# The fused third pass of a two-layer graph and mixture-of-experts kernel: another order of its steps

## The chip, the cores and the metric

The kernel runs on one core of one Trainium2 chip. The metric is the device time in microseconds (us) of one execution; lower is better.

## The reference

The input is 8192 tokens of 256 numbers (128 graphs of 64 nodes). Two layers follow each other, and each has a graph part and an expert part; both add to the running x:

```python
# layer 0
x = x + gnn0(layernorm(x), adj)              # adjacency, two dense layers
h = layernorm(x)                             # 64 experts, six for each token
x = x + layernorm(h + out_w @ mix(h)) * g + b
# layer 1
h = layernorm(layernorm(x))
x = x + relu((adj @ h) @ W_rel + b_rel + h @ W_root) + layernorm(x)   # the layer adds its own input
n = layernorm(x)
top2 = softmax(top_k(n @ Wg + bg, 2))        # 8 experts, two for each token
x = x + sum(top2[e] * ffn_e(n))
```

## The kernel before, in words

The work is done in four stages. The first computes the graph part of layer 0 and sends each token's row to a table in DRAM, six times, to the place of its expert. The second goes through that table in pages of 128 rows, multiplies each by its expert's matrix and scatters the products to the array r0y. The **fused pass**, which the change touches, gathers them again and does the rest of layer 0, all of layer 1's graph part, and the choice of experts of layer 1. The fourth stage goes through the table r1x, which the fused pass fills, in pages of 256 rows.

The fused pass works on 32 blocks of 256 tokens, each held as two tiles of 128 partitions. Its functions for a block b are:

- `load_y` (line 1010, two DMAs of 768 KB: the six products of each token) and `load3` (lines 1018, 1020, 610: xn1 and x1 of layer 0, 256 KB each, and the adjacency blocks).
- `fold` (line 1051, DVE) adds the last two of the six products to the first two; for blocks 0 to 7 it does nothing, and six are summed on PE in place of four. `mixture` (line 1030) sums and transposes the products on PE, 16 matmuls (24 in blocks 0 to 7), and ScalarE (ACT) copies the result out as accT (line 1033). `out_proj` (lines 1038, 1041) multiplies by out_w into po.
- `output` (A, 20 small steps): h = po + xn1 (line 1069), its statistics (lines 56, 59), a square root on ACT (line 36, bn_sd), a reciprocal (line 1075), the normalized h (1079), x2 (1083), its statistics, two more roots (std), reciprocals (1096 to 1101), and on ACT the tiles hn (1105) and s (1110). `bias_x1` (1116) prepares x1.
- `flip_h` (line 89 with hn; ACT hT, line 1125), `neighbours` (1133, pz; ACT z, 1136), `convolve_a` (1141, 1144, pc) and `convolve_b` (1150, pc): the graph part of layer 1 on PE.
- `residual` (R, 9 steps): x3 = max(pc, 0) + s (line 1156) and its store to the output (1157), its statistics, a root on ACT, reciprocal and shift (1164, 1166), and on ACT the normalized rows xs (1170).
- `flip3` (line 89 with xs; ACT xn3T, 1178) and `gate1` (1184, pg): the logits of layer 1's choice.
- `choice` (H, 7 steps): logits (1190), the two largest and their places (217, 220), the marks hot (223, 226). `compare1` (line 315, on POOL) writes each row's destination into column D of xs. `count1` (line 240) counts the marks on PE into pos, and `slots` (S, 6 steps, lines 343 to 362) turns counts into rows of the table.
- `place1` and `send1`: a difference of logits on DVE (line 319) and an indirect DMA of 128 rows from POOL (line 369), four per block. `load_w2` (1199) fetches the fourth stage's weights, one expert in each of eight steps.

`staggered` runs a list of pairs (lag, function): in step s it calls each function, in the order of the list, for block s - lag. So one step works on up to nine blocks at once, and the list is the order in which instructions stand on PE, DVE and ACT: `tc.manual_schedule` at the head of the kernel keeps the written order on these three. On SP and POOL, which issue the DMAs, the order is made by the scheduler from the same program. `chain` makes a generator of A, H, R and S, so that each mention in the list does one small step of it. Each engine works through its instructions in order and waits at the first that is not ready.

Buffers that matter: pc, po, pz, pg and pos have one PSUM buffer each; y, xn1, x1, x3, s and xs have three, accT and hn two, hT, z, h and xn3T one. An xs tile is written again only when the four sends of the block three before it have landed.

Of the kernel before, what the change touches and what calls it, by code (L numbers as in the profile page):

```python
# [520 lines left out]
def staggered(n, stages, first=0):  # L521

    for s in range(first + min(lag for lag, _ in stages), n + max(lag for lag, _ in stages)):
        for lag, f in stages:
            if first <= s - lag < n:
                f(s - lag)
# [3 lines left out]
def two_layer_gnn_moe_kernel(ctx: ExitStack, tc: tile.TileContext, a: dict, out: bass.AP):  # L530
# [452 lines left out]
    with tc.tile_pool(name="c3", bufs=1, reuse_waits="tile") as c3, \  # L983
# [69 lines left out]
        def chain(make):  # L1053

            name = make.__name__

            def advance(b):
                B = blocks[b]
                if name not in B:
                    B[name] = make(b)  # L1060
                next(B[name])

            return advance
# [148 lines left out]
        def send1(b, i):  # L1212

            B = blocks[b]
            t, k = i // 2, i % 2
            r1.differ(t, k, B["top"], B["xs"])
            r1.send(B["row"], B["xs"], b > NB // 2, (k,), (t,))

        A, H, R, S = chain(output), chain(choice), chain(residual), chain(slots)
        staggered(NB, (  # L1220
            (-4, load_y),
            (-2, load3),
            (3, H),
            (0, A),
            (3, H),
            (3, H),
            (0, A),
            (3, H),
            (-2, mixture),
            (0, A),  # L1230
            (3, H),
            (0, A),
            (3, H),
            (1, flip_h),
            (0, A),
            (0, A),
            (3, H),
            (3, compare1),
            (3, count1),
            (2, R),  # L1240
            (4, lambda b: send1(b, 1)),
            (0, bias_x1),
            (2, R),
            (0, A),
            (2, R),
            (-1, out_proj),
            (0, A),
            (2, R),
            (0, A),
            (2, R),  # L1250
            (2, R),
            (0, A),
            (0, A),
            (4, lambda b: send1(b, 2)),
            (0, A),
            (2, R),
            (0, A),
            (2, R),
            (2, R),
            (1, neighbours),  # L1260
            (0, A),
            (3, S),
            (0, A),
            (0, A),
            (3, S),
            (4, lambda b: send1(b, 3)),
            (-3, fold),
            (3, S),
            (1, convolve_a),
            (0, A),  # L1270
            (3, S),
            (0, A),
            (3, S),
            (2, flip3),
            (0, A),
            (3, S),
            (1, convolve_b),
            (2, gate1),
            (3, place1),
            (0, A),  # L1280
            (4, load_w2),
        ))
        r1.page_table(work.tile([P, 512], F32, name="scratch", bufs=1))
# [110 lines left out]
```

## Time and profile before

| what | us |
|---|---|
| median of three runs | 2300.91 |
| fastest and slowest of them | 2292.11, 2304.97 |
| the profiled execution, its own time | 2296.33 |
| its span, first to last instruction | 2294.2 |
| line 1069 (h) of the first and of the last block | 1396.9, 1733.4 |
| busy in the span: PE, PEld, DVE, ACT, POOL | 1983.8, 1694.9, 1159.5, 1004.5, 1167.9 |

PE is TensorE's matmuls and PEld its weight loads, DVE is VectorE, POOL is GpSimd; SP issues most of the DMAs and computes nothing. A matmul's recorded end is modelled, so a busy PE is not one at its peak, and distances between starts tell more. In a line of a timeline stand the start, the length, engine, line, operation, out<-in with sizes, the count, and in brackets the idle time before it with what ended it. A wait for several semaphores is put down to the one that came last by the profile. "Landing" is the time at which a DMA's data has arrived and its semaphore says so.

The fused pass takes from about 1374 us (its first y loads) to about 1763 us (the last count). Between two blocks' line 1069 lie mostly 10.9 us; in the first steps, where the pipeline fills and mixture has 24 matmuls, 7.6 to 12.0.

### The profile page before, as it was taken

Reading aid. Unit: us, or ns where it says so; the run is one execution under the profiler, and the core shown is the slowest. Engines: PE = TensorE matmul, PEld = TensorE weight load, DVE = VectorE, ACT = ScalarE, POOL = GpSimd, SP = SyncE. Lnnn points to the kernel's source line nnn. Section 1 sums busy time; section 2 is a strip of 40 time slices with the busy share of each in tenths; the row PEclk is TensorE's granted clock in tenths of the full one; section 3 lists DMA queues with packets and bytes.
Section 4 is the critical chain, followed back from the end, with each engine's and each line's share of the span. In section 5 each row is a group of like instructions: output and inputs, shape, how many; then the busy total and the mean of one; then the engine's idle time right before and its main releaser. Section 6 shows DMA issues by size and latency. Waiting matters only on the chain. (4 is left out here: it accounts for less than half of the span.)

```text
span 2294.2 us, 36714 instructions
## 1 busy us (share of the span) xinstructions
PE 1983.8 (86%) x10324; PEld 1694.9 (74%) x10324; DVE 1159.5 (51%) x4165; ACT 1004.5 (44%) x2033; POOL 1167.9 (51%) x1134
## 2 busy tenths in 40 slices
PE   7989888889884777887888777999997999999996
PEld 6877767777773566666766666888886888888885
DVE  6878877777885222222222224788886222222221
ACT  5867766667761121111112113666664333333332
POOL 0456655556566656656666660344444444444443
PEclk9999999999996899988899989999998999999998
DMA  3334444443355877755555418898852766667674
GB/s 111 104 109 135 140 134 132 144 134 131 119 172 196 235 237 218 206 169 175 174 177 172 143 62 323 293 319 294 286 196 89 176 160 164 163 162 161 158 166 98
DMA packets 282557, 397.87 MB, mean 173 GB/s; under 512 B 56024, under 2 KB 236392, under 8 KB 282352
## 3 DMA queue, kind: packets, MB, share of 16 engines
q1 hardware_dynamic: 202880, 246.61, 36.5%
q0 software_dynamic: 64416, 136.14, 19.9%
q10 hardware_dynamic: 15056, 12.69, 1.7%
q8 instruction: 92, 1.51, 0.3%
q14 instruction: 113, 0.93, 0.1%
HBM read 222.84 MB, written 176.64 MB: 174 GB/s over the span
## 5 line engine op out<-in xcount | busy, mean ns | idle before, releaser
L369 POOL DMA_INDIRECT r0x<-xs,r0row x384 | 398.1, 1037 | 335.2 <-DVE xs L328 133.4
L954 PE MATMUL py<-lat,pxT 128*128 x1616 | 426.9, 411 | 115.7 <-ACT pxT L941 80.0
L376 POOL DMA_INDIRECT r0y<-px x404 | 391.8, 970 | 229.0 <-DVE px L958 111.2
L954 PEld LDWEIGHTS py<-lat,pxT 128*128 128x128 f32 x1616 | 317.2, 207 | 171.3 <-ACT pxT L941 90.4
L958 DVE TENSOR_SCALAR px<-py,px 128x256 f32<-128x256 f32 x404 | 170.8, 479 | 448.2 <-remote 175.8
L386 POOL DMA_INDIRECT out_x<-py_s,px x138 | 215.5, 1562 | 296.5 <-DMA out_x<-py_s,px 242.0
L941 ACT COPY pxT<-pt 128x512 f32<-128x512 f32 x202 | 113.8, 588 | 519.3 <-remote 220.5
L1332 ACT ACTIVATE phid<-ph,pw 128x256 f32<-128x256 f32 x276 | 130.6, 473 | 321.1 <-issue 167.7
L1330 PE MATMUL ph<-pxT,pw 128*128 128x256 f32 x1104 | 251.1, 381 | 0.7 <-ACT pxT L1321 0.7
L1350 PE MATMUL py<-fw,phid 128*128 (+1 forms) x1104 | 249.8, 379 | 0.1
L753 PE MATMUL ps<-lat 128*128 128x256 f32 x1024 | 247.2, 392 | 0.0
L720 PE MATMUL ph<-lat 128*128 128x256 f32 x1024 | 236.9, 389 | 7.7 <-issue 4.7
L1330 PEld LDWEIGHTS ph<-pxT,pw 128*128 128x128 f32 x1104 | 210.8, 191 | 30.0 <-ACT pxT L1321 1.1
L720 PEld LDWEIGHTS ph<-lat 128*128 128x128 f32 x1024 | 196.8, 195 | 37.7 <-issue 9.9
L1350 PEld LDWEIGHTS py<-fw,phid 128*128 128x128 f32 x1104 | 204.5, 190 | 25.3 <-issue 0.3
L753 PEld LDWEIGHTS ps<-lat 128*128 128x128 f32 x1024 | 200.0, 198 | 27.2
L369 POOL DMA_INDIRECT r1x<-xs,r1row x128 | 136.2, 1064 | 129.6 <-ACT hn L1105 50.4
L939 PE MATMUL pt<-ident,px 128*128 128x128 f32 x808 | 130.4, 284 | 12.4 <-DMA px<-r0x 7.6
L939 PEld LDWEIGHTS pt<-ident,px 128*128 128x128 f32 x808 | 106.8, 148 | 37.2 <-issue 14.2
L723 ACT ACTIVATE lat<-ph,c_L_gnn_b 128x256 f32<-128x256 f32 x256 | 101.3, 471 | 65.0 <-PE ph L720 34.1
L1353 DVE TENSOR_TENSOR py_s<-py,pb 128x512 f32<-128x512 f32 x69 | 47.7, 691 | 156.3 <-PE py L1350 145.1
L1344 DVE TENSOR_SCALAR p<-p 128x2 f32<-128x2 f32 x69 | 12.4, 180 | 225.7 <-ACT p L1343 225.7
(307 smaller groups left out, 2932.5 us busy)
## 6 DMA issues: line engine op xcount, KB each, us to landing
px<-r0x SPq DMA_DIRECT2D x404, 129.0 KB
y<-r0y SPq DMA_DIRECT2D x64, 768.0 KB
pw<-in_L_ffn_W1b SPq DMA_DIRECT2D x69, 514.0 KB
px<-r1x SPq DMA_DIRECT2D x69, 258.0 KB
x<-x SPq DMA_DIRECT2D x64, 256.0 KB
pb<-in_L_ffn_b SPq DMA_DIRECT2D x69, 128.0 KB
r0x<-r0filler ACTq DMA_DIRECT2D x64, 129.0 KB
lat<-in_x SPq DMA_DIRECT2D x32, 256.0 KB
```

What stands on the lines that cost most here:

```text
L369: i = self.nc.gpsimd.indirect_dma_start(out=self.table[:, :], out_offset=bass.IndirectOffsetOnAxis(ap=row[:, t, k:k + 1], axis=0), in_=xs[ ...
L376: d = self.nc.gpsimd.indirect_dma_start(out=self.answer[:, :], out_offset=bass.IndirectOffsetOnAxis(ap=x[:, self.D:self.D + 1].bitcast(I32 ...
L386: i, d = f"{self.name}add{i}", self.nc.gpsimd.indirect_dma_start(out=self.total[:, :], out_offset=bass.IndirectOffsetOnAxis(ap=x[:, self.D ...
L720: nc.tensor.matmul(ph[:, c, :], lhsT=w1[:, k, ts(2 * j + c, P)], rhs=B["aggT"][:, k, :], start=(k == 0), stop=(k == KD - 1))
L753: nc.tensor.matmul(B["po"][:, t, :], lhsT=B["hT"][:, c, ts(t, P)], rhs=w2[:, c, :], start=False, stop=(t == T - 1 and c == KH - 1))
L939: nc.tensor.transpose(pt[:, k, ts(q, P)], Q["px"][:, q, ts(k, P)], ident)
L941: nc.scalar.copy(xT[:, :, :n * P], pt[:, :, :n * P])
L954: nc.tensor.matmul(py[:, q, :], lhsT=xT[:, k, ts(q, P)], rhs=lat[:, ds(regs["e"][(2 * j + q) % 4], 1), k, :].rearrange("p o d -> p (o d)") ...
L958: nc.vector.tensor_scalar(px[:, q, :D], py[:, q, :], px[:, q, D + 1:D + 2], None, op0=ALU.mult)
L1330: nc.tensor.matmul(ph, lhsT=w[:, k * F1 + c * P:k * F1 + (c + 1) * P], rhs=Q["xT"][:, k, :], start=(k == 0), stop=(k == KD - 1))
L1332: nc.scalar.activation(hid[:, c, :], ph, AF.Relu, bias=w[:, KD * F1 + c:KD * F1 + c + 1], scale=1.0)
L1350: nc.tensor.matmul(py[:, t, :], lhsT=Q["hid"][:, c, ts(t, P)], rhs=fw2[:, ds(e, 1), c, :].rearrange("p o d -> p (o d)"), start=(c == 0), s ...
```

## The change

Only the list given to `staggered` is different. No function, lag or buffer is changed, so each block does the same work, in the same step; what changes is the order within a step. Before, a step began with the choice (H) of block s - 3 mixed with output (A) of block s, then the residual (R) of block s - 2, then the slots (S). After, R and A begin the step; H begins about a third of the list later; count1 stands behind convolve_a; S comes at the end. On ACT the roots of R and A (line 36) stand ahead of the copies accT and hT, which they followed before. load3 is called ahead of load_y.

```diff
--- before.py
+++ after.py
@@ -1218,66 +1218,66 @@
 
         A, H, R, S = chain(output), chain(choice), chain(residual), chain(slots)
         staggered(NB, (
+            (-2, load3),
             (-4, load_y),
-            (-2, load3),
+            (2, R),
+            (0, A),
+            (2, R),
+            (2, R),
+            (0, A),
+            (2, R),
+            (2, R),
+            (2, R),
+            (0, A),
+            (4, lambda b: send1(b, 1)),
+            (0, A),
+            (0, A),
+            (0, A),
+            (0, bias_x1),
+            (2, R),
             (3, H),
-            (0, A),
+            (2, R),
+            (0, A),
+            (-2, mixture),
+            (1, flip_h),
+            (2, R),
+            (-1, out_proj),
             (3, H),
+            (0, A),
             (3, H),
             (0, A),
             (3, H),
-            (-2, mixture),
             (0, A),
             (3, H),
             (0, A),
+            (4, lambda b: send1(b, 2)),
             (3, H),
-            (1, flip_h),
-            (0, A),
             (0, A),
             (3, H),
             (3, compare1),
+            (0, A),
+            (1, neighbours),
+            (0, A),
+            (0, A),
+            (0, A),
+            (4, lambda b: send1(b, 3)),
+            (1, convolve_a),
             (3, count1),
-            (2, R),
-            (4, lambda b: send1(b, 1)),
-            (0, bias_x1),
-            (2, R),
-            (0, A),
-            (2, R),
-            (-1, out_proj),
-            (0, A),
-            (2, R),
-            (0, A),
-            (2, R),
-            (2, R),
-            (0, A),
-            (0, A),
-            (4, lambda b: send1(b, 2)),
-            (0, A),
-            (2, R),
-            (0, A),
-            (2, R),
-            (2, R),
-            (1, neighbours),
+            (-3, fold),
             (0, A),
             (3, S),
-            (0, A),
-            (0, A),
-            (3, S),
-            (4, lambda b: send1(b, 3)),
-            (-3, fold),
-            (3, S),
-            (1, convolve_a),
             (0, A),
             (3, S),
             (0, A),
             (3, S),
             (2, flip3),
-            (0, A),
-            (3, S),
             (1, convolve_b),
             (2, gate1),
+            (0, A),
+            (3, S),
+            (3, S),
+            (3, S),
             (3, place1),
-            (0, A),
             (4, load_w2),
         ))
         r1.page_table(work.tile([P, 512], F32, name="scratch", bufs=1))
```

More of the change, by code (lines that the diff above doesn't have):

```diff
@@ L1220, in two_layer_gnn_moe_kernel @@
         staggered(NB, (
+            (-2, load3),
             (-4, load_y),
-            (-2, load3),
-            (3, H),
-            (0, A),
-            (3, H),
-            (3, H),
-            (0, A),
-            (3, H),
-            (-2, mixture),
-            (0, A),
-            (3, H),
-            (0, A),
-            (3, H),
-            (1, flip_h),
-            (0, A),
-            (0, A),
-            (3, H),
-            (3, compare1),
-            (3, count1),
-            (2, R),
-            (4, lambda b: send1(b, 1)),
-            (0, bias_x1),
-            (2, R),
-            (0, A),
-            (2, R),
-            (-1, out_proj),
-            (0, A),
             (2, R),
@@ L1252, in two_layer_gnn_moe_kernel @@
             (0, A),
+            (2, R),
[8 more added lines that the diff above has]
+            (2, R),
+            (3, H),
+            (2, R),
[4 more added lines that the diff above has]
+            (-1, out_proj),
+            (3, H),
+            (0, A),
+            (3, H),
+            (0, A),
+            (3, H),
+            (0, A),
+            (3, H),
             (0, A),
             (4, lambda b: send1(b, 2)),
+            (3, H),
             (0, A),
-            (2, R),
+            (3, H),
+            (3, compare1),
             (0, A),
-            (2, R),
-            (2, R),
             (1, neighbours),
             (0, A),
-            (3, S),
             (0, A),
             (0, A),
+            (4, lambda b: send1(b, 3)),
+            (1, convolve_a),
+            (3, count1),
+            (-3, fold),
+            (0, A),
             (3, S),
-            (4, lambda b: send1(b, 3)),
-            (-3, fold),
-            (3, S),
-            (1, convolve_a),
             (0, A),
@@ L1274, in two_layer_gnn_moe_kernel @@
             (2, flip3),
+            (1, convolve_b),
+            (2, gate1),
             (0, A),
             (3, S),
-            (1, convolve_b),
-            (2, gate1),
+            (3, S),
+            (3, S),
             (3, place1),
-            (0, A),
             (4, load_w2),
```

## The prediction

> **What bounds the kernel now.** I read first the busy shares by stretch and where the fused pass lies. The source view of line 1069, which works once per block (min/median/max ns, then first and last start), puts the pass at 1397 to 1733 us, and the stretches inside it read (length, then busy us of PE, PEld, DVE, ACT, POOL, the clock, the DMA share, GB/s):
>
> ```profile
> L1069 DVE TENSOR_TENSOR h<-po,xn x32: 680/681/692, 1396.9 to 1733.4; 128x512 f32<-128x512 f32 x32
> 1462.60:1573.10 110.50, 107.44 (x668) 91.35 (x667) 94.07 (x455) 69.36 (x152) 49.02 (x50) 1.00 0.94 318
> 1582.20:1679.50 97.30, 94.63 (x587) 80.48 (x586) 83.02 (x407) 61.11 (x134) 39.52 (x46) 1.00 0.85 282
> ```
>
> No compute engine is full: PEld has gaps, DVE is at 0.85. The DMA share is 0.94 while expert weights are fetched too, 0.85 after. Then the chain of waits, which shows one step as one closed line:
>
> ```profile
> 1502.27 0.81 PE pg L1184 x8
> 1503.10 0.17 DVE logits L1190
> 1503.28 0.60 DVE h L1069
> ...
> 1505.23 0.14 DVE r1hot L226
> 1505.37 0.60 DVE x L1156
> ...
> 1510.73 0.81 ACT xs L1170
> 1511.59 0.55 PE ps L89 x3
> 1512.13 1.05 PE pc L1150 x4
> 1513.18 0.81 PE pg L1184 x8
> 1514.01 0.17 DVE logits L1190
> ```
>
> The reader is to see that logits returns after 10.91 us, and that the line passes from the gate (pg) through the whole choice on DVE, then residual and norm, to the copies xs on ACT and back to PE. The residual needs only pc, but stands on DVE behind the choice, which needs pg. What this costs PE is in the timeline of PE:
>
> ```profile
> 1526.53 0.60 PE L89 MATMUL ps<-ident,hn 128*128 128x128 f32 x4
> 1527.25 0.19 PE L240 MATMUL pos<-r1hot,r0tri 128*128 128x16 bf16 x2
> ...
> 1532.96 0.27 PE L89 MATMUL ps<-ident,xs 128*128 128x128 f32 x1
> 1533.41 0.55 PE L89 MATMUL ps<-ident,xs 128*128 128x128 f32 x3 [0.18 <-ACT xs L1170]
> 1533.88 1.13 PE L1150 MATMUL pc<-z,at 128*128 128x256 f32 x4
> ```
>
> By distances between starts in that timeline, PE's own work per step is: count 0.10, out_proj 1.94, neighbours 1.73, convolve_a 1.94, four transposes 0.45, convolve_b 0.86, gate 0.81, sixteen transposes 1.79, four transposes 0.45. The sum is 10.07 us; the other 0.84 of the 10.91 are waits for r1hot, xs and z.
>
> **The change, part by part.** No computation is added or removed: PE, DVE and ACT have the same instructions in another order.
>
> *Residual first, choice later.* x3 now stands on DVE right behind pc; logits stands 3.7 us later, and pg is long done. I add the new line from the end of convolve_b, each term a start-to-start distance of the DVE timeline: x3 0.60, h 0.60, two statistics of x3 0.66, one of h 0.33, two aggregates 0.20, the other of h 0.33, a difference 0.07, an aggregate 0.10 and a last one 0.17: 3.06. The root follows at 0.05 and takes ACT 0.20, the copy accT 0.50, hT 1.02: 4.83. Then PE, with 0.05 for the handover: neighbours 1.73, convolve_a 1.94, count 0.10, four transposes 0.45: 9.10; convolve_b 1.05 to its recorded end and 0.05 to the next x3: **10.20 us**. Everything else is off this line. xs on ACT starts at 4.72 and its transposes stand at 8.65; hot is ready at 6.54 and count stands at 8.54; z is copied from 6.82 for 9.10. Since count moves on PE behind out_proj, neighbours and convolve_a, the slots on DVE wait 0.55 for it; behind them stand one more root's reciprocal and the next x3, which waits for pc 0.30 longer anyway. The same sums over the old order close at 10.83 where 10.91 is measured, so I carry the missing 0.08: 10.28, a gain of 0.63 a step. PE then waits 0.14 for hT.
>
> *Roots ahead of the copies.* In a full step this is a cost: the root waits on ACT for DVE's statistics (3.11), and behind it are queued accT and hT, which neighbours waits for; that is the 0.14. At the start of the pass it is a gain: DVE stood idle 2.64, 1.33 and 1.68 us at line 1075 in the first steps, since the root was queued behind a copy that waits for the transposes. The copy itself is only 0.58, but it came late; I take 2 us for the fill.
>
> *Moved transfers.* SP's order is made by the scheduler, and the instruction list of the changed program shows it: adjacency and y's halves keep together, but x1 (line 1020), which waits for the x2 that frees its buffer, now stands ahead of at least one y half. x2 ends at 5.9 of the step, so y goes out at about 6.4 where it went at 3.9. Its fold is two steps later at 7.1, over 20 us on: hidden. If that cover were gone each late us would be one a step. The first y's stand behind two 256 KB loads: 0 to 2 us at the start, where PE waits for y; po of the first step covers it, I take 0.
>
> *The sends.* POOL writes column D of xs (line 315) only when four older sends have landed, then issues four; ACT's xs waits for the same landing. The landing is not in before's chain, but the new step leaves it less room. POOL's timeline:
>
> ```profile
> 1499.43 1.97 POOL L369 DMA_INDIRECT r1x<-xs,r1row  x1 [0.30 <-issue]
> 1501.71 0.97 POOL L369 DMA_INDIRECT r1x<-xs,r1row  x1 [0.30 <-DVE rs L1096]
> ...
> 1518.22 0.53 POOL L315 TENSOR_SCALAR xs<-r1dest 128x4 int32<-128x4 f32 x1 [4.63 <-DMA r1x<-xs,r1row]
> ...
> 1752.10 0.22 POOL L315 TENSOR_SCALAR xs<-r1dest 128x4 int32<-128x4 f32 x1 [0.43 <-DMA r1x<-xs,r1row]
> ```
>
> One turn of this loop is line 315 with its gap 0.75, four sends at about 1.28, and the landing counted from the end of the last send. While weights are fetched line 315 starts at 1462.63 and, ten turns on, at 1573.11: 11.05 a turn, with no wait for DVE in it. From 1582 to 1680 the landing is 2.0 to 5.5, mostly under 4, and sends wait up to 2.4 for DVE. Between these ends (a fixed 11.05 a turn: no gain in 11 steps; a landing that shrinks with its burst: no cost) I take 0.3 us in each of 11 steps, nearer to the second, because line 315 kept to 3 to 5 us after logits all along, so that the landing follows the y burst and not the sends; in the new step xs can be 2.3 late (to 7.0) before z and PE feel it.
>
> The Trainium skill, *DMA: Bandwidth & Descriptors*, section "Queues, rings and completion order", says that a DMA engine alternates between queue rows packet by packet; by that, sends would not stand behind y, the 0.3 would be nothing and the sum 3 us lower. The trace speaks against it: the wait is 4.63 us beside y and, in the empty end, 1752.10 less 1750.40 (the end of the last send it waits for), 1.7 us.
>
> **The sum**, against the profiled execution (2296.33 us; span 2294.2): 24 full steps at 0.63 are 15.1; three early steps of 24 transposes go from 11.49 to 10.07 + 0.89 + 0.08 = 11.04, 1.3; fill 2; the tail, where R no longer waits for H in two or three thinning steps, 2; less 11 times 0.3, 3.3. That is 17.1 saved: **2279 us**. The runs shown have a median of 2300.91, 4.6 above the profiled one, and spread from 2292 to 2305; I keep 2279.
>
> **Rivals.**
> - *The landing binds while weights are fetched.* Those 11 steps stay at 11.05, 0.77 over 10.28: 8.5 lost in place of 3.3, so 2284. For it: ten turns at 11.05. Against: the landing's lock to the burst.
> - *A new wait takes the old one's place.* On the new line DVE's statistics, the roots and hT are in series with PE, where before PE had spare work. If DVE's part is 0.7 longer than I sum (its starts depend on each other, or h waits for xn1), the step is 10.91 again; fill and tail leave 4: 2292, no change. For it: accT and hT stand behind the root in every step. Against: every term is a row. That the listed order isn't what runs would give 2296, but the instruction list shows it moved.
> - *Slower: the send loop sets every step.* The last send of a block is released right ahead of fold on DVE; a send beside fold took 1.97 against 0.97 (above; fold ran from 1499.34). With 1.0 more and a landing of 5.5 in all steps, since y now goes out among the sends, a turn is 0.75 + 5.1 - 0.3 + 1.0 + 5.5 = 12.05; 27 steps at this against a mean of 10.97 are 29 more, less 4: 2321. It decides from a landing of 4.4 on (a turn over 10.91). For it: 4.3 to 5.9 while weights are fetched. Against: 3.2 to 4 later.
>
> **Chances.** Forecast 0.50, the landing in a third 0.20, no gain 0.17, the slow loop 0.13. About 0.5% (11.5 us of 2300.9) is what a measurement of this kernel can tell from no change: the first two lie under 2289.4, faster 0.70; same 0.17; slower 0.13. Low end: PE without any wait, 27 times 0.84 and 4 for the ends, 2269, less 4 for a quick run: 2265. High end 2302: it takes in the no-gain case with the runs' own spread and leaves out the slow one.
>
> **What would show it.** Right: L1069 starts every 10.2 to 10.4 us; logits without a wait for pg; x3 waiting about 0.3 for pc; waits for r1hot and xs gone from PE, a short one for hT at L1133; line 315 still waiting for DMA with L1170 not waiting for it. Wrong: L1170 waiting for DMA or POOL, turns of line 315 over 11 us, mixture or fold waiting for y, or L1133 waiting 0.5 or more for hT.

## The result and the profile after

The changed kernel takes **2287.98 us** (median of 9 runs, 2276.4 to 2298.7), the kernel before 2298.5 beside it (9 runs, 2292.1 to 2308.6): a ratio of **0.9947**, with a 95% interval of 0.9922 to 0.9972. The forecast was 2279; the median lies 9 us above it and 4 above the 2284 of the rival in which the landing binds. The profiled execution took 2284.81 us, with a span of 2283.0.

The source view of line 1069 and then two stretches of the fused pass, of the changed kernel (columns as in the prediction):

```profile
L1069 DVE TENSOR_TENSOR h<-po,xn x32: 677/680/692, 1402.2 to 1725.8; 128x512 f32<-128x512 f32 x32
```

```profile
1480.00:1580.00 100.00, 96.02 (x596) 80.91 (x596) 84.06 (x406) 63.09 (x138) 41.34 (x46) 1.00 0.94 307
1580.00:1680.00 100.00, 99.72 (x647) 87.13 (x646) 91.63 (x446) 67.66 (x148) 47.22 (x50) 1.00 0.91 305
```

From first to last start line 1069 now takes 323.6 us in place of 336.5. In the second stretch PE is busy for 99.72 of 100 us, where it had 97% in the two stretches before; in the first, while expert weights are fetched, it still has gaps. The chain of waits of the changed kernel shows the border between the two (start, length, what):

```profile
1599.90 0.80 ACT xs L1170
...
1602.24 0.97 POOL r1x L369
1603.52 0.97 POOL r1x L369
1604.80 4.69 DMA r1x<-xs,r1row
1610.31 0.80 ACT xs L1170
...
1623.91 0.92 PE pg L1184 x8
1624.83 1.80 PE ps L1030 x16
...
1627.29 1.73 PE po L1041 x8
1629.01 1.73 PE pz L1133 x8
...
1630.95 1.73 PE pc L1144 x8
...
1633.26 0.86 PE pc L1150 x4
1634.12 0.92 PE pg L1184 x8
```

From 1618 on it is PE alone, and pg returns after 10.21 us: no choice, no norm, no copy in it. Before 1610 it is another loop, which does not stand in the old chain (that has one landing from 1440 to 1740 us, ahead of line 362): xs, the sends, 4.69 us from the start of the last send's issue until it has landed (3.7 from the issue's end), and xs of a later block, which may not overwrite its buffer sooner. That wait, and two that the prediction named, in the changed kernel from 1450 to 1700 us (total us, times, longest):

```profile
POOL xs L315 <- DMA r1x<-xs,r1row: 41.6, 8, 5.8
ACT xs L1170 <- DMA r1x<-xs,r1row: 19.2, 9, 3.8
PEld pz L1133 <- ACT hT L1125: 6.1, 20, 0.7
PEld ps L89 <- ACT xs L1170: 4.6, 9, 1.1
```

And one long step, from the timelines of ACT and of POOL:

```profile
1500.85 1.52 ACT L1170 ACTIVATE xs<-x,bn_nm,bn_rs 128x512 f32<-128x512 f32 x2 [2.23 <-DVE xs L319]
1502.28 0.56 ACT L1136 COPY z<-pz 128x512 f32<-128x512 f32 x1
```

```profile
1494.93 0.96 POOL L369 DMA_INDIRECT r1x<-xs,r1row  x1 [0.30 <-DVE x L1156]
1500.92 1.20 POOL L315 TENSOR_SCALAR xs<-r1dest 128x4 int32<-128x4 f32 x1 [5.04 <-DVE xs L319]
```

ACT and POOL start within 0.1 us of each other, 5 us after the last send's issue ended: one event released both. The brackets name whatever DVE ended nearby (its one-element write goes to another block's buffer); the chain names the landing. How much room xs has, from a step of the kernel before and from a quiet step (one that no landing lengthens) of the changed kernel:

```profile
1507.75 0.55 POOL L315 TENSOR_SCALAR xs<-r1dest 128x4 int32<-128x4 f32 x1 [5.07 <-DVE h L1079]
1510.01 1.52 ACT L1170 ACTIVATE xs<-x,bn_nm,bn_rs 128x512 f32<-128x512 f32 x2 [1.37 <-DVE r1run L343]
```

```profile
1665.47 0.68 DVE L1069 TENSOR_TENSOR h<-po,xn 128x512 f32<-128x512 f32 x1
...
1669.48 1.52 ACT L1170 ACTIVATE xs<-x,bn_nm,bn_rs 128x512 f32<-128x512 f32 x2
```

Before, xs started 6.7 us after h (1510.01 less 1503.28) and line 315 2.3 us ahead of xs, so the landing did not hold xs. Now xs is ready to start 4.0 after h, and where the landing is later than that it is xs that waits, then z behind it on ACT, and PE.

Where the 15.2 us went that the pass (first load of y to last count) is shorter in these two profiles, 389.1 to 373.9: the 24 full steps (seventh h to thirty-first) 262.0 to 254.2, the start up to the seventh h 85.9 to 83.1, the end 41.2 to 36.6. The span differs by 11.2, because the stages ahead of the pass, which the change does not touch, took 5.5 longer in the second execution and what follows the pass 1.5 less.

### The profile page after: what moved, and what is told of

Read it like the earlier page. It is cut to its first block, busy times and chain, and to the rows that moved or that the text cites. A ratio compares the mean times of both kernels' runs of the same rounds, so it can differ in the third digit from the quotient of the medians.

```text
span 2283.0 us, 36780 instructions
## 1 busy us (share of the span) xinstructions
PE 1975.4 (87%) x10324; PEld 1692.3 (74%) x10324; DVE 1162.4 (51%) x4165; ACT 1007.1 (44%) x2033; POOL 1171.0 (51%) x1134
```

## Experiments

**Theory A**: a full step is the longer of PE's work, 10.21 us, and a loop of sends and landing, and the changed kernel loses the difference while weights are fetched. **Theory B**: there the DMA engines are full, and any order gives 11 us. The runs are from three other chips, on which the kernel before takes 2048 to 2050 us (the stages ahead of the pass are some 250 us shorter; the steps of the pass are the same), so only ratios, each to the kernel before on the same chip, compare with the result above. In the table, "full" is the sum of the 24 full steps (24 times 10.21 is 245.0), "start" runs from the first load of y to the seventh h, "end" from the last but one h to the last count, all from one profile each; the ratio is that of the median times to the kernel before, with its 95% interval.

| kernel | full | start | end | pass | ratio |
|---|---|---|---|---|---|
| before, four xs | 261.8 | 89.0 | 40.4 | 391.2 | 0.9998 (0.9984 to 1.0012) |
| before, root ahead | 262.1 | 87.0 | 39.5 | 388.5 | 0.9997 (0.9986 to 1.0007) |
| changed | 255.8 | 86.4 | 36.6 | 378.8 | 0.9932 (0.9918 to 0.9946) |
| changed, copies ahead | 265.5 | 86.2 | 34.9 | 386.5 | 0.9931 (0.9908 to 0.9954) |
| changed, y ahead | 247.8 | 86.8 | 36.6 | 371.2 | 0.9899 (0.9882 to 0.9916) |
| changed, y and copies ahead | 252.2 | 86.8 | 34.8 | 373.7 | 0.9932 (0.9910 to 0.9954) |
| changed, weights late | 245.7 | 85.9 | 38.2 | 369.8 | 0.9907 (0.9892 to 0.9922) |
| changed, four xs | 245.4 | 85.6 | 36.6 | 367.6 | 0.9890 (0.9875 to 0.9905) |
| the same again | 245.4 | 87.0 | 36.6 | 368.9 | 0.9907 (0.9891 to 0.9922) |
| four xs, copies ahead | 245.0 | 86.7 | 33.1 | 364.7 | 0.9874 (0.9856 to 0.9892) |
| the same again | 245.0 | 87.0 | 34.8 | 366.7 | 0.9883 (0.9869 to 0.9897) |
| four xs, y and copies ahead | 244.9 | 87.3 | 33.1 | 365.2 | 0.9878 (0.9862 to 0.9893) |

### A fourth buffer of xs

```diff
-            B["xs"] = xs = work.tile([P, T, 2, W], F32, name="xs", bufs=3)
+            B["xs"] = xs = work.tile([P, T, 2, W], F32, name="xs", bufs=4)
```

> The changed kernel with four buffers of xs in place of three. Theory A (in the 12 full steps in which expert weights are fetched, 8th to 19th of 24, what sets 11.0 us is the landing of the four sends of three blocks earlier, which ACT's xs and POOL's line 315 wait for): with a fourth buffer both wait for sends a whole step older, so those 12 steps fall from a mean of 11.00 to 10.2 to 10.4, the waits of xs and of line 315 for DMA go from 19 and 42 us to under 5, the 24 full steps take 246 to 250 us in place of 254.2, and the time is 2277 to 2281. Theory B (the DMA engines themselves are full there, share 0.94 to 1.00, and every transfer comes late): the 12 steps stay at 10.8 or more, another wait (for y, at or x1) takes the place, and the time is within 3 us of the changed kernel's 2288.

The full steps are 10.21 but for one group of 10.90, 9.89 and 10.09, which begins where DVE once looks at the counts for the first pages (lines 170 to 176); a group like it stands in every run of the new order. From 1190 to 1480 us xs waits for no landing and line 315 for 2.4 us in all. The weights are fetched as before, and the stretch in which they are reads:

```profile
1220.00:1320.00 100.00, 100.00 (x647) 88.47 (x646) 92.26 (x442) 68.51 (x150) 46.57 (x49) 1.00 1.00 335
```

The DMA share is 1.00, at 335 GB/s, and PE has no gap. So B falls: full DMA engines alone cost nothing here; what cost was that xs had to wait for a transfer issued one step earlier. The same edit in the kernel before:

> The kernel before with four buffers of xs. Theory A (its 10.91 us come from the line pg, choice, x3, norm, xs, pc, pg, in which the landing is no term): steps stay at 10.91 (10.88 to 10.95), the time within 0.3% of the kernel before. Theory B (the 10.91 hold a landing too, so the new order gained only by moving it): steps under 10.8 in the part in which weights are fetched, 1 to 3 us faster.

Steps stay at 10.90 to 10.94 and the ratio holds 1: as A has it, the landing was no term there.

### The weights later

```diff
+                nc.vector.tensor_copy(fw2[:, e, 0, 0:1], blocks[e + 24]["x2"][:, 0, 0:1])
                 nc.sync.dma_start(out=fw2[:, e], in_=a["L1_ffn_W2"][e].rearrange("(k p) d -> p k d", p=P))
...
-            (4, load_w2),
+            (24, load_w2),
```

> The changed kernel, but the eight 512 KB loads of the second expert weights wait for x2 of blocks 24 to 31 (through a copy of one element a partition on DVE, 0.07 us each), so that they go out near the end of the pass, where the DMA share is 0.27 to 0.66; three buffers of xs as in the changed kernel. Theories A and B agree here: without these loads the steps in which they ran fall to 10.2 to 10.4, and only some 4 to 5 steps beside the three loads of the first pages' weights (which move up) stay near 11; 5 to 7 us less in the pass, 2281 to 2284 if the end of the pass doesn't wait for the late weights. Theory C (it isn't the traffic but the place in the pass, such as more experts being full): the long steps stay where they are, 2288.

The long steps go with the loads: two are left, 10.84 and 11.03, fewer than the four or five expected, and the second is that of the look at the counts. The gain on the changed kernel (0.9932 to 0.9907 is 5 us) is in the range; the pass is 9.0 us shorter in these profiles, more than the 5 to 7 expected, though its end is 1.6 longer. So the place in the pass is not what makes the landing late. But the run does not price the weights alone, because SyncE's order changed with them (h of this step stands at 1233.4):

```profile
1235.67 0.92 SPq L1010 DMA_DIRECT2D y<-r0y  x2
1238.66 0.37 SPq L1020 DMA_DIRECT2D x<-x  x1
```

In the first four full steps y goes out 2.1 to 2.8 us after h here (one half at 5.7), where the changed kernel has 5.7 and 6.2. What that place of y is worth with the weights beside it is seen two sections on.

### The changed kernel beside them

> The changed kernel, unaltered, beside the kernel before on the chip of these runs, so that the other versions have it as their neighbour. Theory A: quiet full steps of 10.21 us, 8 to 13 steps of a mean of 10.8 to 11.2 while weights are fetched, ratio to the kernel before 0.992 to 0.997, and so 0.4 to 0.8% behind the version with four buffers of xs (0.989). If the gain of the fourth buffer came from elsewhere (another chip), this ratio is 0.989 to 0.990 as well and there are no long steps.

Nine full steps of 10.6 to 13.2 us, the others between 9.9 and 10.2; 10.7 us over 245.0, where the first profile has 9.1. What the fourth buffer gained is not the chip's.

### The order of the two loads

```diff
-            (-2, load3),
             (-4, load_y),
+            (-2, load3),
```

> The changed kernel with load_y listed ahead of load3 again, as before; in SyncE's order both halves of y then stand ahead of xn1 and x1. Theory A1 (the sends land when the burst they stand behind ends, so that its place in the step matters): y leaves some 2 us earlier, the burst ends earlier, and the steps in which weights are fetched fall from 11.0 to 10.2 to 10.6: 4 to 8 us less than the changed kernel. Theory A2 (the amount fetched per step alone delays the sends, at whatever place): those steps stay at 10.8 to 11.2, and the time is within 2 us of the changed kernel. In both, quiet steps stay at 10.21.

SyncE's timeline, first of the changed kernel (h of this step at 1244.4), then with y ahead (h at 1253.4):

```profile
1249.67 0.36 SPq L1020 DMA_DIRECT2D x<-x  x1
1250.12 0.89 SPq L1010 DMA_DIRECT2D y<-r0y  x2
```

```profile
1255.52 1.00 SPq L1010 DMA_DIRECT2D y<-r0y  x2
1256.62 0.56 SPq L1018 DMA_DIRECT2D xn<-xn  x1
1258.68 0.37 SPq L1020 DMA_DIRECT2D x<-x  x1
```

In the changed kernel y waits behind x1 and goes out 5.7 us after h (both halves in the first four full steps, one half in the next six, none later), with y ahead at 2.1. The full steps then lose 2.8 us in place of 10.7: A1, and the time is 8 us less. The amount fetched is the same, so its place decides. The order of these two loads, a side line of the change, costs most of what is lost to the landing. The run with the weights late has y in nearly this place and loses 0.6, so what the weights add with y ahead is about 2.2.

### The two copies ahead of the two roots

```diff
             (0, A),
+            (-2, mixture),
+            (1, flip_h),
             (2, R),
             (2, R),
             (2, R),
...
             (0, A),
-            (-2, mixture),
-            (1, flip_h),
             (2, R),
             (-1, out_proj),
```

> The changed kernel with the mixture and the flip of hn listed ahead of the two roots again: ScalarE's order is accT, hT, two roots, xs as before; DVE's, PE's and SyncE's orders stay those of the changed kernel. Theory A (DVE is at 0.92 of a step, so a root that comes behind two copies stalls it): hT no longer keeps PE waiting (6 us in all), but the roots come some 1.5 us later, DVE waits 0.5 to 1.5 us a step for them, quiet steps are 10.5 to 11.0 in place of 10.2, and the fill is 1 to 2 us longer: 2291 to 2300. Rival (the place of the roots does nothing, the order of residual and choice alone makes the gain): quiet steps of 10.1 to 10.25, within 3 us of 2288.

Theory A of this expectation missed: quiet steps are 10.21 all the same. DVE does wait for the later root, but has the room, and the long steps come from the landing; from 1200 to 1440 us of this run:

```profile
ACT xs L1170 <- DMA r1x<-xs,r1row: 35.6, 11, 5.8
DVE bn_rs L1164 <- ACT bn_sd L36: 22.4, 20, 3.6
```

Its profiled execution was the slowest of its five (2048.2; the others 2031 to 2044), so the 20.5 us over 245.0 are not its usual loss; the median is the changed kernel's. Two of its long steps (13.59 and 13.00, one after the other) come over 60 us after the last weights were asked for, behind a send that landed 6.8 us after its issue; why that one was late is open. With four buffers, where no landing disturbs:

> The changed kernel with four buffers of xs and the two copies ahead of the two roots on ScalarE again. The run with three buffers and the copies ahead kept 10.21 in its quiet steps, though DVE waited about 1 us a step for the later root. Theory A (a later root only delays xs, and that costs where the landing of the sends has eaten the slack of xs): with the fourth buffer all 24 full steps are 10.21 to 10.25 and the ratio to the kernel before is that of four buffers with the roots ahead, 0.989 within 0.0015. Rival (the later root costs by itself, by DVE's waits): steps of 10.4 and more, ratio 0.992 or more.

The full steps are 10.21 on the mean (one group of 11.12, 9.67 and 9.85 among them), although DVE waits for that root again (1190 to 1480 us):

```profile
DVE bn_rs L1164 <- ACT bn_sd L36: 22.0, 26, 1.8
```

It came out ahead of roots first, so the two ran again on one chip.

> The changed kernel with four buffers of xs once more, as neighbour on one chip of the same with the copies ahead of the roots. Theory A: steps 10.21 in both, so all that the place of the roots moves is the ends: 2 to 4 us of the tail in favour of the copies ahead (33.1 against 36.6 from the start of the last block's h step to the last count, on two chips), ratio 0.988 to 0.990. Rival (the place of the roots is of no account in the ends either): the two within 1 us.

> The changed kernel with four buffers of xs and the copies ahead of the roots once more, beside the one with the roots ahead. Theory A: 2 to 4 us (0.001 to 0.002) faster than roots ahead, ratio 0.9865 to 0.988. Rival: the same within 1 us.

2029.4 and 2025.0 us: 4.4 in favour of the copies ahead, though the intervals of the two ratios overlap a little. The ends of the pass favour them by 1.8 to 3.5 us. The roots ahead of the copies bring nothing in any full step and probably cost a little at the end. In the kernel before, with the two copies behind the root of h alone:

> The kernel before with the mixture and the flip of hn listed behind the root of h: one root, accT, hT, the other root, xs on ScalarE; the choice still ahead of the residual on DVE. Theory A (the line through gate, choice, residual, norm and xs sets 10.91, and the roots are no term of it that this moves): full steps stay at 10.88 to 10.95, the fill is 0 to 2 us shorter, ratio 0.999 to 1.001. Rival (the place of the roots is a good part of the gain): steps of 10.5 to 10.8 and a ratio of 0.995 to 0.998.

Full steps of 10.90 to 11.00, ratio 0.9997: nothing there either. The root does move the start: its last two steps with 24 matmuls are 11.05 each, against 11.48 and 11.49 in the kernel before with four xs, and the start is 2.0 shorter in these two profiles, too little for the ratio to tell.

### The new order of residual and choice alone

This kernel has both edits above: y ahead, and the copies ahead of the roots.

> One part of the change alone, with three buffers of xs: the residual ahead of the choice (and the places of counts, sends and slots that go with it); y's loads ahead of xn1 and x1 as before, and the two copies ahead of the two roots as before. Theory A (this part takes the line under PE's own 10.21 us and makes the whole gain; what is left over is the landing of the sends, which y's early place shortens and the later root lengthens, since xs has less room): quiet full steps 10.21, an excess over 24 times 10.21 between that of y ahead (2.8 us) and that of copies ahead (10 to 20 us), ratio 0.989 to 0.992, between 1 us slower and 8 us faster than the changed kernel. Rival (the roots ahead of the copies are needed for the gain): quiet steps over 10.4, ratio 0.995 or more.

What is left of the change is the residual ahead of the choice, and the places of the counts, the sends and the slots that go with it. Ratio 0.9932, the whole change's own: this one part makes the whole gain, with 7.1 us lost to the landing in its profile. That is more than the 2.8 of y ahead alone; the later root leaves xs less room, but only 0.3 us (in the quiet steps of the runs with four buffers xs ends 2.25 us ahead of its transposes on PE, with the roots ahead 2.54), so why the loss is larger is open, and the two medians (2034.7 and 2028.3) are from two chips. With four buffers too:

> The same part alone, with four buffers of xs: the candidate for the fastest version. Theory A: all full steps 10.21, pass of 364 to 366 us, ratio 0.986 to 0.989, within 0.0015 of copies ahead with four buffers (0.9874) and not behind roots ahead with four buffers.

2024.8 us, 9.9 less than with three buffers on the same chip, and full steps of 10.20 on the mean. The three runs with four buffers and the copies ahead lie at 0.9874 to 0.9883 and can't be told apart: 23 to 27 us under the kernel before, and about 0.5% under the changed one.

## Why the prediction was right, point by point

- **The closed line through the choice set 10.91.** Confirmed: neither a buffer nor the root moves that step; the residual ahead of the choice takes it away.
- **The new step.** Forecast 10.28, from a line of 10.20; measured 10.21. The size was right, its reason not quite: I had PE's own work at 10.07 and a wait of 0.14 for hT. PE's own work is 10.21 (gate 0.92 in the new chain where I read 0.81, four transposes 0.49 where I read 0.45), and with four buffers PE is busy without a gap whether or not the roots stand ahead. What the line of x3, norm, root and hT takes stays just hidden: in the quiet step at 1664.86 x3 waits 0.18 for pc, where I forecast about 0.3.
- **The sends' landing.** This is the term that was mis-sized: 3.3 us, measured 9.1 (254.2 less 245.0), and 10.7 on another chip. My rival of a landing that binds, with 8.5, was nearer, and the sign named for it, L1170 waiting for DMA, is there. I took a value near the lower end because line 315 kept 3 to 5 us behind logits, so that the landing follows the burst. It does; but the burst was moved too. The step "y goes out at 6.4, hidden" had the time right (5.7 after h is 6.3 of the step), but looked at y's fold, 20 us on, and not at the sends beside y: with y back ahead of xn1 and x1, 7.9 of the 10.7 us are gone. Two readings were too even: line 315 kept 3 to 5 us only while weights are fetched, and one landing there took 2.97 us, under the 4.3 given as the least.
- **The Trainium skill's rule** (*DMA: Bandwidth & Descriptors*, section "Queues, rings and completion order"), from which I drew that sends alternate packet by packet with y and so cost nothing: these traces disagree with that conclusion again. In the changed kernel the last send lands 3.4 to 6.6 us after its issue while weights are fetched, and 1.7 in the empty end. How packets alternate the traces do not show, so the rule itself is left open.
- **The start.** Forecast 1.3 for the early steps and 2 for the fill, measured 1.3 and 1.4 on the first chip. I put the fill down to the roots, and that is not shown: with the copies ahead the start is 86.2 against 86.4, but in the kernel before a root ahead brought 2.0. One kernel's start differs by 1.4 between its two runs (four xs, 85.6 and 87.0), so single profiles cannot tell the causes apart.
- **The end.** Forecast 2, measured 4.6 (and 3.8 against the kernel before with four buffers).
- **The sum.** Forecast 17.1, measured 15.2 in the pass of this pair of profiles: 5.8 more lost to the landing and 0.6 less won at the start, against 1.9 more from the steps (10.21 for 10.28, 10.92 for 10.91) and 2.6 more at the end. That these nearly cancel is luck. The medians differ by 10.5 us on this chip and by 13.8 on the chip on which the two kernels ran again.
- **The other rivals.** No gain: did not come, L1133's waits for hT are 0.3 each. The slow loop at 12.05 a turn in all steps: turns of up to 12.5 came, but only while weights were fetched; afterwards they were 8.9 to 10.6.

## What to carry to other kernels

An order that makes a writer earlier eats the slack of the buffer it writes: ask who still reads that buffer, transfers too, and how many steps ago they were issued. One more buffer, worth nothing before the reordering (0.9998), was worth 5 to 10 us after it. And a load that is only moved is priced by what lands beside it in its new place, not only by when its own reader wants it.

## What the runs showed of the hardware

- DMA engines at a share of 1.00 (335 GB/s over 100 us) held up no step, once xs waited for no transfer of the step before.
- In the changed kernel the last send of a block took 3.4 to 6.6 us from its issue's end until its buffer was free while weights were fetched, against 1.7 in the empty end of the pass.
- The same y loads, sent out up to 3.6 us later in the step, took the loss to that landing from 2.8 to 10.7 us over 24 steps.
- The same program's stages ahead of the pass took 1379 us on the first chip and 1127 on another, at a mean granted clock of 0.946 and 0.973. Single operations last as long on both (the copy of line 941 has a median of 585 ns on each), and the steps of the pass are the same 10.21; why those stages differ is open.
